# Projecting layer 3's context keys and values inside layer 1's context attention, and fetching them from DRAM batch by batch

## The chip, the cores and the metric

One Trainium2 chip; the kernel runs on one of its cores. The metric is the device time of one execution in microseconds, a median of several runs. A core has five engines, each with its own instruction queue that it works off in order: TensorE (PE, matrix products, whose weight loads the profile lists apart as PEld), VectorE (DVE), ScalarE (ACT), GpSimd (POOL) and SyncE (SP, which here only issues DMAs). TensorE reads from the on-chip memory SBUF and writes to the eight banks of PSUM; DVE and ACT copy results out of PSUM.

## The reference

The program is a decoder of four layers on x of 8 batches x 256 tokens x 256 features (float32). Each layer is x = layernorm(x + f(x)) three times: a self mixing, an attention to a context, and a feed-forward part. The context, `ctx_768`, is 8 batches x 120 tokens x 192 features and is the same for all layers; nothing in the network changes it. Two of the twelve parts matter here, and both attend to that context:

```python
def _L1_xattn_ref(...):   # 16 heads of 16, in layer 1
    q = x @ w_q + b_q;  k = context @ w_k + b_k;  v = context @ w_v + b_v
    ... softmax(q k^T / 4) v, then @ w_o + b_o

def _L3_xattn_ref(x, context, Wq, Wk, Wv, Wo, bo):   # 8 heads of 64, in layer 3
    q = (x @ Wq)...; k = (context @ Wk)...; v = (context @ Wv)...
    attn = softmax(q k^T * 64 ** -0.5)
    return (attn @ v) @ Wo + bo
```

Layer 3's keys and values depend on the context and on two weights (192 x 512 each) alone, so they can be computed at any time after these are loaded.

## The kernel before, in words

The parts run one after another over the same activations X (128 tokens by 256 features, 16 such tiles) and their transpose xT. `build` loads the weights of a part while the part ahead of it runs: there are two weight buffers that take turns, every load is issued on SP's queue, and it waits there until the buffer's last reader is done. The kernel is written as nested Python functions; the order in which they call an engine is the program order, and a scheduler may move an instruction in its engine's queue where it foresees a wait. So it is an in-order queue per engine that sets what runs when.

**Layer 1's context attention** (`l1_xattn`, from about 755 to 932 us of the profiled execution). `project` makes queries, keys and values of two batches at a time. Then `attention16` (L632) goes through the eight batches as a software pipeline. In the turn of batch b, TensorE computes the scores of b with keys as rows (`exps16`; ACT takes their exponentials, L556) and, in between, the scores of b + 1 with queries as rows (`largest16`; DVE takes their maxima into `low`, L501). The output projection of batch b - 1 lies between the first and second step. DVE and POOL then normalise batch b - 1 into X (L622, L167, L145, L147, L191), TensorE turns the maxima (L536, `lower16`) and the fresh X (L177, the turn), and `choose` computes the next part's gate logits and writes X to DRAM (L744, for the gathers of the mixture of experts that follows). Last come the weighted sums of b (L605). PSUM is handed out by `bank`, which goes round eight banks, six called `sc` and two `pt`. `attention16` has a hook, `ready`: three functions, of which the third gives, for a batch, an early, a late and a last step to be put into its turn. Layer 2's self attention uses it; layer 1's context attention doesn't.

**Layer 2's feed-forward part with layer 3 woven in** (`l2_ffn`, from about 1560 to 2440 us). Per batch, `experts` projects hidden units (PE), then gathers 64 x 128 rows of a table from DRAM by indirect DMAs that POOL issues one by one (L953), four at a time into one of four row buffers. DVE forms a dot product of each with X (L1480), ACT makes diagonal matrices of the weights (L1531) and PE adds the weighted rows up (L1532). At fixed places the loop takes one step, `next(later, None)`, of a chain of generators: the routing of the next batch, and layer 3's convolution and context attention (`convolve`, `attend`) of the batch before. What is left of the chain at the end of a batch is run before the batch is finished. The chain of the last batch, `convolve(7)` and `attend(7)`, is emitted after the loop and overlaps layer 3's feed-forward part (`fixed_point`), which ends the program. The weights of that last part (2 MB) are loaded on SP's queue between the loop and this chain.

`attend` is `context_batches` (L1609). Its first step for batch b adds the bias to X and computes keys and values: eight products of a 128 x 128 weight block with the 120 context columns into one PSUM tile, and two products of the context with 512 columns of weights into another. The second step copies them to SBUF, the keys on ACT (L1635), the values on DVE (L1636) beside a column of ones that POOL wrote once. Then follow queries, scores (L1656), exponentials, transposes (L1672), weighted sums with the column of ones giving the softmax's denominator (L1678), the output projection (L1696) and the norm.

The line numbers here and in the profile are those of the listing:

Of the kernel before, what the change touches and what calls it, by code (L numbers as in the profile page):

```python
# [11 lines left out]
F32 = mybir.dt.float32  # L12
# [8 lines left out]
P = 128  # L21
B, S, D = 8, 256, 256
NT = B * S // P
NTOK = B * S
SC, DC = 120, 192
# [17 lines left out]
class Net:  # L43
    def __init__(self, ctx: ExitStack, tc: tile.TileContext, ins, out):
        self.tc, self.nc, self.ins, self.out = tc, tc.nc, ins, out
        nc = self.nc
        self.const = ctx.enter_context(tc.tile_pool(name="const", bufs=1))
        self.wpool = ctx.enter_context(tc.tile_pool(name="weights", bufs=1))
        self.tmp = ctx.enter_context(tc.tile_pool(name="tmp", bufs=3))
        self.ps_t = ctx.enter_context(tc.tile_pool(name="ps_t", bufs=2, space=PSUM))  # L50

        self.ident = self.const.tile([P, P], F32, name="ident")
        make_identity(nc, self.ident)
        self.ones = self.const.tile([1, P], F32, name="ones")
        nc.gpsimd.memset(self.ones, 1.0)

        self.X = self.const.tile([P, NT, D], F32, name="X")
        self.xT = self.const.tile([P, 2, NTOK], F32, name="xT")
        self.xT4 = self.xT.rearrange("p c (t n) -> p c t n", n=P)
        for b in range(B):  # L60
            nc.sync.dma_start(
                self.X[:, 2 * b : 2 * b + 2, :],
                ins["x"][b].rearrange("(t p) d -> p t d", p=P),
            )
        self.cols = self.const.tile([P, ins["cols"].shape[1]], F32, name="cols")
        nc.scalar.dma_start(self.cols, ins["cols"])
        self.consts = self.const.tile([P, ins["consts"].shape[1]], F32, name="consts")
        nc.scalar.dma_start(self.consts, ins["consts"])
        self.earlier = self.const.tile([P, P], BF16, name="earlier")
        nc.vector.tensor_copy(self.earlier, self.cst("earlier"))  # L70
        self.causal = self.const.tile([P, P], BF16, name="causal")
        nc.vector.tensor_scalar(self.causal, self.cst("later"), -1e30, None, ALU.mult)

        self.later_k = self.const.tile([P, P], BF16, name="later_k")
        nc.vector.tensor_scalar(self.later_k, self.cst("sooner"), -1e30, None, ALU.mult)
        self.other = self.const.tile([P, P], BF16, name="other")
        nc.vector.tensor_scalar(self.other, self.cst("other"), -1e30, None, ALU.mult)
        self.ident_bf = self.const.tile([P, P], BF16, name="ident_bf")
        nc.vector.tensor_copy(self.ident_bf, self.ident)
        self.ones_bf = self.const.tile([P, P], BF16, name="ones_bf")  # L80
        nc.gpsimd.memset(self.ones_bf, 1.0)
        self.ctxT = self.const.tile([P, 2, NCTX], F32, name="ctxT")
        nc.scalar.dma_start(self.ctxT, ins["ctxT"].rearrange("p (c n) -> p c n", c=2))
        self.gate1 = self.const.tile([P, 2, 32], F32, name="gate1")
        nc.scalar.dma_start(self.gate1, ins["l1f_gate"].rearrange("p (c n) -> p c n", c=2))
        self.avg = self.const.tile([P, 2, B], F32, name="avg")

        self.x_max = self.const.tile([P, B], F32, name="x_max")
        self.w_scale = self.const.tile([P, len(L2X)], F32, name="w_scale")
        self.half = self.const.tile([P, 2], F32, name="half")  # L90
        nc.gpsimd.memset(self.half, -0.5)
        self.power = False
        dram = ctx.enter_context(tc.tile_pool(name="dram", bufs=1, space=bass.MemoryType.DRAM))

        self.xd1 = dram.tile([NTOK + 1, D], F32, name="xd1")

        self.yd1 = dram.tile([32 * 256 + 1, D], F32, name="yd1")
        self.one = self.const.tile([P, 1], F32, name="one")
        nc.gpsimd.memset(self.one, 1.0)
        self.wset = 0  # L100
# [609 lines left out]

    def load_l1_xattn(self):

        *w, spare = self.load(*((f"l1x_w{n}", 2) for n in "qkvo"), rows=("l1x_bv", "l1x_bo"), spare=16 * NT + 8)
        top = spare[:, : 16 * NT].rearrange("p (a t k) -> p a t k", a=2, k=8)
        self.top1, self.top1_i, self.w_sums = top[:, 0], top[:, 1].bitcast(U32), spare[:, 16 * NT :]
        return w

    def l1_xattn(self, w):
        nc = self.nc
        wq, wk, wv, wo, bv, bo = w  # L720
        with ExitStack() as ctx:
            work, low, vps = self.attn16_pools(ctx, "x1", SC, 1)
            bv, bo = self.everywhere(bv, work, "bv"), self.everywhere(bo, work, "bo")

            def project(b, vp):
# [27 lines left out]
                    nc.vector.max(self.top1[:, i, :], lg[:, j, :])  # L753
                    nc.vector.max_index(self.top1_i[:, i, :], self.top1[:, i, :], lg[:, j, :])

            self.attention16(project, low, vps, [SC], False, wo, bo, work, then=choose)

            o = 0
            for j, (_, k, n, _) in enumerate(L2X):
                n *= k // P  # L760
                for a in range(0, n, 2048):
                    m = min(2048, n - a)
# [653 lines left out]
    def l2_ffn(self, w):  # L1416


        tc = self.tc
        with ExitStack() as ctx:  # L1420
            w3 = self.load(
                ("l3a_win", 2), ("l3a_wout", 2), *((f"l3x_w{n}", 4 if n == "o" else 2) for n in "qkvo"),
                rows=("l3a_bout", "l3a_ln_w", "l3a_ln_b", "l3x_bo"),
            )
            win, wout, wq, wk, wv, wo, bout, ln_w, ln_b, bo = w3
            pool3 = ctx.enter_context(tc.tile_pool(name="a3", bufs=1))
            ps3 = ctx.enter_context(tc.tile_pool(name="a3p", bufs=2, space=PSUM))
            convolve = self.convolution_batches((win, wout, bout, ln_w, ln_b), pool3, ps3)
            attend = self.context_batches((wq, wk, wv, wo, bo), pool3, ps3)
            later = iter(())  # L1430
            with (
                tc.tile_pool(name="f2", bufs=1) as pool,
                tc.tile_pool(name="f2w", bufs=2) as work,
                tc.tile_pool(name="f2p", bufs=2, space=PSUM) as ps,
            ):
                experts = self.expert_batches(w, pool, work, ps)
                for b in range(B):
                    experts(b, later)
                    later = chain(convolve(b), attend(b))
            w4 = self.load(("l3f_w1", 2), ("l3f_w2", 8), rows=("l3f_b2",))  # L1440
            pool = ctx.enter_context(tc.tile_pool(name="f3", bufs=1))
            work = ctx.enter_context(tc.tile_pool(name="f3w", bufs=3))
            ps = ctx.enter_context(tc.tile_pool(name="f3p", bufs=2, space=PSUM))
            for _ in later:
                pass
            self.power = True
            self.fixed_point(w4, pool, work, ps)
# [161 lines left out]
    def context_batches(self, w, pool, ps):  # L1609

        nc = self.nc
        wq, wk, wv, wo, bo = w
        HD = 64
        v1 = pool.tile([SC, 8, HD + 1], F32, name="v1")
        nc.gpsimd.memset(v1[:, :, HD : HD + 1], 1.0)
        half = [slice(0, HD), slice(HD, 2 * HD)]
        out_bias = pool.tile([P, D], F32, name="out_bias")
        pp = ps.tile([P, D], F32, name="s")
# [3 lines left out]
        def batch(b):  # L1622
# [1 line left out]
            nc.vector.tensor_tensor(  # L1624
                z, self.X[:, 2 * b : 2 * b + 2, :], out_bias.unsqueeze(1).to_broadcast([P, 2, D]), ALU.add
            )
            ctxT = self.ctxT[:, :, b * SC : (b + 1) * SC]
            kT = pool.tile([P, 4, SC], F32, name="kT")
            pk = ps.tile([P, 4, SC], F32, name="s")
            for m in range(4):  # L1630
                self.mm(pk[:, m, :], [(wk[:, c, m * P : (m + 1) * P], ctxT[:, c, :]) for c in range(2)])
            pv = ps.tile([P, 512], F32, name="s")
            self.mm(pv[:SC], [(ctxT[:, c, :], wv[:, c, :]) for c in range(2)])
            yield
            nc.scalar.copy(kT, pk)  # L1635
            nc.vector.tensor_copy(v1[:, :, :HD], pv[:SC].rearrange("p (h d) -> p h d", d=HD))  # L1636
            qT = pool.tile([P, 4, S], F32, name="qT3")
            for m in range(0, 4, 2):
                pq = ps.tile([P, 2, S], F32, name="s")
# [594 lines left out]
```

## Time and profile before

| | |
|---|---|
| median of 3 runs | 2679.72 us (2677.69 to 2682.74) |
| the profiled execution | 2687.66 us, its span 2685.9 us |
| TensorE | 2173.3 us busy, 81% of the span, mean granted clock 0.884 |
| VectorE, ScalarE, GpSimd | 60%, 37%, 35% of the span |
| DMA traffic | 135.05 MB, 50 GB/s on average |
| layer 1's context attention, 755 to 932 us | PE 145.83 us busy of 177, granted clock 0.80 |
| the loop of layer 2's feed-forward part, 1600 to 2440 us | PE 657.60, DVE 564.54, POOL 514.74, ACT 344.09 us busy of 840; clock 0.88 |
| 2440 to 2530 us | PE 67.62 us busy of 90; clock 0.72 |

Busy times of TensorE come from modelled ends of pipelined products, and a product of float32 operands shows as two records. The granted clock is the share of full speed that the chip gave TensorE: at 0.50 a product takes twice as long. "Idle before" in a group of instructions is how long their engine had nothing to do just ahead of them, with the instruction that ended the wait. "Issue" is time in which the profile shows nothing that the engine waited for, and "remote" or "another core or an unknown queue" is a wait that ended by something not in the trace.

### The profile page before, as it was taken

The page shows a single profiled execution, that of the slowest core. Times are in us where ns is not written, and L with a number is a line of the kernel's source. Part 1 is how long each engine was busy: PE and PEld are TensorE (multiplying, and loading weights), DVE is VectorE, ACT ScalarE, POOL GpSimd, SP SyncE. Part 2 cuts the span into 40 slices and gives each one's busy share as a digit, 9 for nine tenths or more (in the row PEclk, how much of TensorE's full clock was granted, in tenths as well). Part 3 has the DMA queues.
Part 4 walks back from the last instruction along what each step waited for, and adds up shares of the span by engine and source line. Part 5 has one row for each costly group of instructions (what it writes and reads, how often), then busy time and mean ns, then how long its engine had stood idle before and what let it go on. Part 6 is the DMA issues. An engine that isn't in the chain of part 4 may idle for free.

```text
span 2685.9 us, 41132 instructions
## 1 busy us (share of the span) xinstructions
PE 2173.3 (81%) x14481; PEld 1569.7 (58%) x14481; DVE 1617.5 (60%) x5506; ACT 992.0 (37%) x2269; POOL 940.5 (35%) x986
## 2 busy tenths in 40 slices
PE   8989789699998689767886877788888778778796
PEld 5656678455565468434454355566667656555575
DVE  4664200566667576346667875757668676654675
ACT  2332233234333442123342433343445434342563
POOL 1021221311111134433210246665566555662122
PEclk9998799799988789878997888889889889887898
DMA  2001431200010137511001021111111111120000
GB/s 84 2 1 56 181 131 57 71 1 1 1 68 13 52 95 224 147 38 32 17 1 59 1 68 48 44 45 42 41 44 43 46 43 42 51 73 14 1 12 20
DMA packets 84173, 135.05 MB, mean 50 GB/s; under 512 B 33445, under 2 KB 53045, under 8 KB 82048
## 3 DMA queue, kind: packets, MB, share of 16 engines
q0 software_dynamic: 52288, 79.27, 10.0%
q1 hardware_dynamic: 28924, 49.45, 5.6%
q10 hardware_dynamic: 2756, 3.72, 0.4%
q8 instruction: 115, 1.88, 0.3%
q14 instruction: 90, 0.74, 0.1%
HBM read 242.90 MB, written 17.70 MB: 97 GB/s over the span
## 4 chain that ended last, share of the span: by engine, by line
PE 38%; DVE 21%; issue 9%; POOL 4%; ACT 4%; another core or an unknown queue 4%; DMA 3%; POOLq 0%; ACTq 0%; DVEq 0%
PE po L1532 5%; PE pp L136 5%; PE s L136 4%; PE sc L136 4%; PE ph L136 2%; DVE low L517 2%; PE sc L484 2%; DMA xe<-xd,take 2%; PE pt L136 2%; DVE low L501 2%; PE sc L605 1%; DVE junk L1480 1%; DVE X L191 1%; PE s L1678 1%
## 5 line engine op out<-in xcount | busy, mean ns | idle before, releaser
L953 POOL DMA_INDIRECT rows<-in_l2f_table_dram,index x512 | 532.8, 1041 | 340.8 <-issue 122.0
L1532 PE MATMUL po<-rows,diag 128*128 128x256 f32 x768 | 226.8, 431 | 92.9 <-ACT diag L1531 62.1
L1480 DVE SCALAR_TENSOR_TENSOR junk<-rows,X 128x256 f32<-128x256 f32 x512 | 214.5, 419 | 57.2 <-DMA rows<-in_l2f_table_dram,index 34.1
L1532 PEld LDWEIGHTS po<-rows,diag 128*128 128x128 f32 x768 | 150.0, 209 | 144.4 <-ACT diag L1531 75.9
L136 PE MATMUL pp<-xT,w 128*128 128x256 f32 (+1 forms) x672 | 196.2, 429 | 26.8 <-issue 21.4
L592 POOL TENSOR_TENSOR aT<-sides,inv 128x256 f32<-128x256 f32 x64 | 46.8, 731 | 431.6 <-DVE sides L590 316.6
L136 PE MATMUL ph<-xeT,we 128*128 128x128 f32 x1248 | 182.7, 289 | 18.3 <-DMA we<-in_l0f_experts_dram,wrow 15.1
L136 PEld LDWEIGHTS ph<-xeT,we 128*128 128x128 f32 x1248 | 168.2, 199 | 38.6 <-DMA we<-in_l0f_experts_dram,wrow 16.4
L1531 ACT ACTIVATE diag<-ident,dots 128x128 f32<-128x128 f32 x384 | 133.8, 394 | 114.7 <-PE po L1532 51.7
L177 PE MATMUL pt<-ident,X 128*128 128x128 f32 x352 | 77.4, 337 | 116.9 <-DVE X L191 93.3
L136 PEld LDWEIGHTS pp<-xT,w 128*128 128x128 f32 x672 | 137.3, 213 | 57.5 <-issue 27.3
L178 ACT COPY xT<-pt 128x512 f32<-128x512 f32 x88 | 51.5, 587 | 302.5 <-PE pt L177 219.0
L953 POOL DMA_INDIRECT xe<-xd,take x87 | 85.2, 979 | 205.3 <-PE pt L968 80.6
L177 PEld LDWEIGHTS pt<-ident,X 128*128 128x128 f32 x352 | 49.6, 165 | 153.1 <-issue 53.1
L136 PE MATMUL py<-we,hT 128*128 128x256 f32 x496 | 129.1, 384 | 0.9 <-DVE hT L1097 0.9
L1074 DVE TENSOR_TENSOR y<-py,we 128x256 f32<-128x256 f32 x23 | 9.8, 424 | 197.6 <-PE py L136 197.6
L556 ACT ACTIVATE e<-sc 128x512 f32<-128x512 f32 (+1 forms) x154 | 81.4, 601 | 103.0 <-PE sc L484 73.9
L1068 ACT ACTIVATE hT<-ph,we 128x128 f32<-128x128 f32 x184 | 65.8, 367 | 119.6 <-PE ph L136 84.9
L484 PE MATMUL sc<-kv,qv 32*128 32x128 f32 (+2 forms) x1448 | 104.2, 320 | 1.7 <-DVE qv L694 0.6
L191 DVE TENSOR_SCALAR X<-z,ln_mv,rs_y 128x256 f32<-128x256 f32 x176 | 68.1, 429 | 58.8 <-POOL rs_y L147 58.4
L136 PE MATMUL s<-xT,w 128*128 128x256 f32 x256 | 72.3, 444 | 38.3 <-issue 26.4
L484 PEld LDWEIGHTS sc<-kv,qv 32*128 32x128 f32 x1448 | 80.2, 190 | 31.2 <-issue 25.9
(535 smaller groups left out, 5204.9 us busy)
## 6 DMA issues: line engine op xcount, KB each, us to landing
we<-in_l1f_experts_dram SPq DMA_DIRECT2D x32, 384.0 KB
yd<-y SPq DMA_DIRECT2D x32, 256.0 KB
rows<-in_l2f_table_dram,index POOLq DMA_INDIRECT x512
w<-in_l2x_w_dram SPq DMA_DIRECT2D x1, 4096.0 KB
yd<-y SPq DMA_DIRECT2D x23, 128.0 KB
X<-in_x_dram SPq DMA_DIRECT2D x8, 256.0 KB
xd<-X ACTq DMA_DIRECT2D x8, 256.0 KB
xd<-X SPq DMA_DIRECT2D x8, 256.0 KB
```

Source lines behind the costliest of these rows:

```text
L136: self.nc.tensor.matmul(out, lhsT=lhsT, rhs=rhs, start=n == 0, stop=n == last and bias is None)
L177: nc.tensor.transpose(pt[:, c, j, :], self.X[:, i0 + j * step, c * P : (c + 1) * P], self.ident)
L191: nc.vector.tensor_scalar(self.X[:, i, :], z[:, j, :], mv[:, j, 0:1], r[:, j : j + 1], ALU.subtract, ALU.mult)
L484: nc.tensor.matmul(sc[: shape[0], part], lhsT=lhsT, rhs=rhs, start=mask is None, stop=True, skip_group_check=True)
L501: nc.vector.tensor_reduce(low5[:, r, :, :, 0], sc, AX.X, ALU.max, negate=True)
L517: nc.vector.tensor_reduce(low4[:, r, :, 0], sc, AX.X, ALU.max, negate=True)
L556: lambda r, sc: nc.scalar.activation(e0[m][:n0, r], sc, AF.Exp),
L953: self.nc.gpsimd.indirect_dma_start(out=out, out_offset=None, in_=table, in_offset=bass.IndirectOffsetOnAxis(ap=index, axis=0), **({} if r ...
L1068: nc.scalar.activation(hT[:, g + f, :], ph[:, f, :], AF.Gelu, bias=b1[:, g + f : g + f + 1])
L1480: nc.vector.scalar_tensor_tensor(junk, row, 1.0, self.X[:, i, :], ALU.mult, ALU.mult, accum_out=out)
L1531: nc.scalar.activation(diag, self.ident, AF.Copy, scale=dots[:, k : k + 1])
L1532: nc.tensor.matmul(po, lhsT=diag, rhs=rows[:, k, D:], start=False, stop=g + k == H * K - 2)
```

## The change

The keys and values of layer 3 are no longer computed in `attend`. Their two weights (512 KB each) are loaded with the weights of layer 1's context attention instead of with layer 3's. In the turn of each batch of layer 1's context attention, as the late step of the hook, a new function `context3` computes the same ten products, copies the keys on ACT and the values on DVE, and writes both to two DRAM buffers from SP's queue (245,760 bytes and 249,600 bytes). The ones beside the values are written by POOL into two buffers once, and travel along. In layer 3, the first step of `attend` fetches both tiles of its batch from DRAM on SP's queue in place of the ten products, and the second step loses both copies.

```diff
+        self.k3 = dram.tile([B, P, 4 * SC], F32, name="k3")
+        self.v3 = dram.tile([B, SC, 8 * 65], F32, name="v3")
...
-        *w, spare = self.load(*((f"l1x_w{n}", 2) for n in "qkvo"), rows=("l1x_bv", "l1x_bo"), spare=16 * NT + 8)
+        *w, spare = self.load(
+            *((f"l1x_w{n}", 2) for n in "qkvo"), ("l3x_wk", 2), ("l3x_wv", 2),
+            rows=("l1x_bv", "l1x_bo"), spare=16 * NT + 8,
+        )
...
+            v3 = [work.tile([SC, 8, 65], F32, name=f"v3{n}", bufs=1) for n in range(2)]
+            for t in v3:
+                nc.gpsimd.memset(t[:, :, 64:], 1.0)
...
+            def context3(b):
+
+                ctxT = self.ctxT[:, :, b * SC : (b + 1) * SC]
+                pk = self.bank([P, 4, P])[:, :, :SC]
+                for m in range(4):
+                    self.mm(pk[:, m, :], [(wk3[:, c, m * P : (m + 1) * P], ctxT[:, c, :]) for c in range(2)])
+                kT = work.tile([P, 4, SC], F32, name="k3")
+                nc.scalar.copy(kT, pk)
+                nc.sync.dma_start(self.k3[b], kT.rearrange("p m s -> p (m s)"))
+                pv = self.bank([P, 512])
+                self.mm(pv[:SC], [(ctxT[:, c, :], wv3[:, c, :]) for c in range(2)])
+                v = v3[b % 2]
+                nc.vector.tensor_copy(v[:, :, :64], pv[:SC].rearrange("p (h d) -> p h d", d=64))
+                nc.sync.dma_start(self.v3[b], v.rearrange("p h d -> p (h d)"))
+
+            def inside(b):
+                return lambda: None, lambda: context3(b), lambda: None
...
-            self.attention16(project, low, vps, [SC], False, wo, bo, work, then=choose)
+            self.attention16(
+                project, low, vps, [SC], False, wo, bo, work, then=choose,
+                ready=(lambda: None, lambda: None, inside),
+            )
...
-                ("l3a_win", 2), ("l3a_wout", 2), *((f"l3x_w{n}", 4 if n == "o" else 2) for n in "qkvo"),
+                ("l3a_win", 2), ("l3a_wout", 2), ("l3x_wq", 2), ("l3x_wo", 4),
...
-        v1 = pool.tile([SC, 8, HD + 1], F32, name="v1")
-        nc.gpsimd.memset(v1[:, :, HD : HD + 1], 1.0)
...
-            ctxT = self.ctxT[:, :, b * SC : (b + 1) * SC]
             kT = pool.tile([P, 4, SC], F32, name="kT")
-            pk = ps.tile([P, 4, SC], F32, name="s")
-            for m in range(4):
-                self.mm(pk[:, m, :], [(wk[:, c, m * P : (m + 1) * P], ctxT[:, c, :]) for c in range(2)])
-            pv = ps.tile([P, 512], F32, name="s")
-            self.mm(pv[:SC], [(ctxT[:, c, :], wv[:, c, :]) for c in range(2)])
+            nc.sync.dma_start(kT, self.k3[b].rearrange("p (m s) -> p m s", m=4))
+            v1 = pool.tile([SC, 8, HD + 1], F32, name="v1")
+            nc.sync.dma_start(v1, self.v3[b].rearrange("p (h d) -> p h d", h=8))
             yield
-            nc.scalar.copy(kT, pk)
-            nc.vector.tensor_copy(v1[:, :, :HD], pv[:SC].rearrange("p (h d) -> p h d", d=HD))
             qT = pool.tile([P, 4, S], F32, name="qT3")
```

In the queues of the built program, TensorE's ten products stand in each turn of layer 1's context attention behind the last of the scores and ahead of the four turns of the maxima (L536), which in the program before had been spread around the turn of X (L177). On SP's queue the two writes of a batch stand ahead of X's write of the batch before it (L744) or near it, and in layer 3 the fetches of batch 7 stand behind the 2 MB of weights for the last part.

## The prediction

> **What bounds the kernel now.** I read first the chain of work that ended last, to see which engines the time hangs on; then the busy time by stretch, for the two parts that the change touches; then the timeline of TensorE in each, for what is idle where work is added and what stands on the chain where work is taken out.
>
> ```profile
> PE 38%; DVE 21%; issue 9%; POOL 4%; ACT 4%; another core or an unknown queue 4%; DMA 3%; POOLq 0%; ACTq 0%; DVEq 0%
> ...
> 1600.00:2440.00 840.00, 657.60 (x2928) 507.51 (x2926) 564.54 (x2770) 344.09 (x899) 514.74 (x495) 0.88 0.17 47
> ```
>
> TensorE carries 38% of the chain, more than any other engine. The second line is the gather loop (length; PE, PEld, DVE, ACT, POOL busy; clock; DMA share; GB/s): PE is busy 78% of it. POOL's 64 gathers per batch of about 1.04 us, with 0.30 us between them, are 86 us of the 107 to 123 us that a batch takes, so POOL is not the bound.
>
> What is moved, seen in batch 0 (PE's timeline, then the two copies by line, min/median/max in ns):
>
> ```profile
> 1736.05 1.94 PE L136 MATMUL s<-ctxT,w 128*128 128x120 f32 x16
> 1737.83 1.88 PE L136 MATMUL s<-w,ctxT 128*120 128x512 f32 x4
> ...
> L1635 ACT COPY kT<-s x8: 559/559/560, 1739.6 to 2523.5; 128x480 f32<-128x480 f32 x8
> ...
> L1636 DVE COPY v<-s x8: 680/692/692, 1741.8 to 2526.1; 120x512 f32<-120x512 f32 x8
> ```
>
> The ten products run from 1736.05 to 1737.83 + 1.88 = 1739.71: 3.66 us at full clock. They lie on the chain itself (start, us, what):
>
> ```profile
> 2188.98 3.69 PE s L136 x20
> ...
> 2303.42 3.69 PE s L136 x20
> ...
> 2426.28 5.28 PE s L136 x20
> ...
> 2519.80 6.29 PE s L136 x20
> ```
>
> Where they arrive, PE stands idle once per batch, ahead of the turn of X, and then runs slow:
>
> ```profile
> 796.63 0.78 PE L177 MATMUL pt<-ident,X 128*128 128x128 f32 x4 [1.46 <-DVE X L191]
> ...
> 816.19 1.12 PE L177 MATMUL pt<-ident,X 128*128 128x128 f32 x4 [3.37 <-DVE low L501]
> ...
> 814.00:816.00 2.00, 0.00 (x0) 0.00 (x0) 2.00 (x5) 0.00 (x0) 0.00 (x0) 0.76 0.32 109
> 816.00:818.00 2.00, 1.81 (x8) 1.81 (x9) 0.71 (x3) 0.59 (x1) 0.00 (x0) 0.50 0.11 35
> 818.00:820.00 2.00, 2.00 (x6) 0.97 (x5) 1.40 (x2) 0.00 (x0) 0.00 (x0) 0.50 0.00 0
> 820.00:822.00 2.00, 2.00 (x17) 1.48 (x20) 0.52 (x6) 0.21 (x1) 0.00 (x0) 0.50 0.00 0
> 822.00:824.00 2.00, 2.00 (x24) 0.97 (x20) 0.97 (x3) 0.06 (x1) 0.00 (x0) 0.50 0.00 0
> 824.00:826.00 2.00, 2.00 (x13) 1.20 (x6) 1.59 (x5) 0.42 (x1) 0.73 (x1) 0.68 0.00 0
> 826.00:828.00 2.00, 2.00 (x9) 1.23 (x8) 1.32 (x5) 1.36 (x3) 0.00 (x0) 1.00 0.00 0
> ```
>
> PE waits 1.46 us or 3.37 us in turn (batch pairs differ in where DVE's maxima lie), and after the gap at 814 the clock stays at 0.50 until about 825.
>
> **The added work, in layer 1's context attention.** Per batch 3.66 us of PE, 0.56 of ACT, 0.69 of DVE and two SP issues of 0.36 us (the row of L744).
>
> PE. The ten products stand just where the gap is. In the turns with the long gap (three) they cost 3.66 - 3.37 = 0.3 us. In those with the short one (three) the four turns of the maxima now stand ahead of X's turn, and need DVE's last maximum, which the trace has done at 799.07; the products end at 794.90 + 3.66 = 798.56, so 0.5 us of waiting comes on top: 3.66 + 0.5 - 1.46 = 2.7. In batch 0 the place is in a stretch at clock 0.50 without a gap: between 3.7 and 7.3, I take 5. In batch 7 the gap is 2.36 us: 1.3. Sum 3 x 0.3 + 3 x 2.7 + 5 + 1.3 = 15.3 us.
>
> The clock. From 796 to 904 us, counting each 2 us stretch's busy time times (1 - clock), PE loses 18 us of work to slow spells, each right behind a gap. Filled gaps should avoid part of them. The Trainium skill (TensorE: Matmul & The Clock Gate, Part 1) says that the clock halves after an idle window of about 3.4 us and returns after about 3.4 us of work. By that rule only the three long gaps go cold, for 3.4 us at half speed each: 3 x 1.7 = 5 us to win, and the part costs 10. The row shows more: a gap of 1.46 us is followed by half clock too (from 798), and the return takes 7 to 10 us. I take half of the 18, 9 us, so the part costs +6. The same rule speaks against the change further on: fewer products in the gather loop leave PE colder.
>
> The copies: ACT's stands behind the exponentials and ahead of xT's copy, which waits for PE anyway; DVE's behind the maxima, while PE is busy with L536. Hidden by PE's own work; bare, 8 x 1.25 = 10 us. SP's writes: X's write (L744) queues near them, but only the gathers of the next part read it, from 965 us, 37 us after the last is issued at 928. POOL's two 0.11 us memsets come before the first batch. The weights' 1 MB is issued at 271 us, behind l1x's 1 MB, which took 270 to 274; DMA is idle until the first expert's fetch at 281.73, so it is through by 278.
>
> Bounds: -3 (all slow spells gone: 15.3 - 18) to +33 (nothing hidden: 8 x 3.66 + 3.7 for the cold batch).
>
> **The removed work, in layer 3.** The chain holds of the products 3.69 us each in batches 3 to 5, 3.05 in batch 1, 1.9 (as an unknown wait) in batch 0 and 2.7 (as "issue") in batch 2: 18.7 us, with about 1.8 us of the copies on the chain 20.5. In the tail, at low clock, 5.28 + 6.29 = 11.6 us. A shorter chain meets the next longest one. In the loop that is ACT, whose longest waits are of another kind:
>
> ```profile
> ACT qT L1473 <- remote: 38.8, 4, 12.2
> ...
> ACT xT L178 <- remote: 31.8, 5, 9.8
> ```
>
> These waits of 5 to 12 us stop PE and DVE as well, end by nothing in the trace, and are not shortened. I take 70% in the loop (14 us): PE feeds itself from one product to the next there, and POOL has 20 us per batch to spare. In the tail I take 60% (7 us), since the next products lose the warm-up that these gave: the clock returns at 2525, at their end. Together -21; bounds -2 and -32.
>
> **The fetches.** Sixteen of 0.25 MB; at the pace of 270 to 274 us (1 MB in 4 us) 1 us each, with a latency as that of the gathers from DRAM on the chain, 3 to 5 us. SP's queue holds nothing else from 1563 to 2399. A fetch waits until the batch before has read its tile: keys are last read at 1800 and next at 1899, values at 1811 and 1907; the nearest pair is 2371 and 2454, the values of batches 5 and 6. Cover of over 80 us against 5. Batch 7's stand behind the last part's weights, which wait for L1513 until 2399, but their own tiles come free only at 2471 and 2478 and are used from 2552. Nothing waits. Without this cover each would cost about 5 us. They share the DMA engines with gathers that DVE waits for (29.7 us in all over the loop): between 0 and 16 us, I take 1. Layer 3's weights shrink by 1 MB at 1557; the first gather at 1576.8 waits for its index, so 0.
>
> **Sum.** +6 - 21 + 1 = -14, against the profiled execution: span 2685.9 to 2672. It took 2687.66 us, 1.8 outside the span, and lies 8 us above the median; the difference carries over: 2679.7 - 14 = 2666 us.
>
> **The rivals.**
> 1. *A wait takes the gap's place (slower).* Between L484 and L177, X's turn now stands behind all four turns of the maxima; if the maxima slip by as much as the products take, the gap stays and the 3.66 us come on top. For it: DVE reduces X and the maxima in one queue, ending 0.5 us behind the products already. Against it: DVE has no other work then. Price +33, less 21: +12, 2692. It decides once a batch costs more than 21 / 8 = 2.6 us net.
> 2. *The removed products were filler.* PE is idle 182 us of the loop, and if ACT's waits or the row buffers set the pace only a third of 32 comes back: -10 + 6 + 1 = -3, 2677, no change.
> 3. *The clock heals.* All slow spells of the attention go and the chain gives 28 us: -3 - 28 = -31, 2649.
> 4. *The fetches collide with gathers*: +15 on the forecast, 2681; in the trace gathers have DMA engines busy 17%, so this is small and goes with rival 2.
>
> **How the numbers follow.** Forecast (2653 to 2674) 0.44; rival 1 0.29; rivals 2 and 4 0.15; rival 3 0.12. 0.2% or 5.4 us is about what a measurement can tell from no change. Faster: forecast and rival 3, 0.56; same 0.15; slower 0.29. The range leaves one in ten on each side: below, rival 3 without its end, 2645; above, rival 1 with part of its worse half, 2697.
>
> **What would show it.** In the changed profile: the wait of L177 for X or the maxima, 20.7 us in all between 750 and 930, falls below 8; the clock of that stretch rises from 0.80 to 0.85 or more, and it grows by 0 to 12 us. L1656 and L1678 never wait for a DMA. The loop from the first gather to the drain shortens by about 14 us, with ACT's remote waits as long as now; the tail by 7. Wrong if the attention grows by over 20 us with L536 waiting for L501 in every turn, or the loop keeps its length.

## The result and the profile after

The kernel after takes 2673.82 us against 2691.98 us of the kernel before, both medians of 20 runs: a ratio of 0.9933, 95% interval 0.9915 to 0.9951, or 18 us faster (13 to 23). The prediction was 2666 us from 2679.7, 14 us faster. The profiled executions differ by 13.3 us of span, 2685.9 to 2672.6. Cut at fixed instructions, the difference lies here (ahead of the first stretch the kernel after is 1.0 us later, where the two differ only in loading two weights):

| stretch (first and last instruction) | before | after | difference | predicted |
|---|---|---|---|---|
| layer 1's context attention (`zero` to the first routing sum) | 177.8 | 171.9 | -5.9 | +6 |
| from there to the first `qT` of layer 2's feed-forward part | 627.5 | 629.9 | +2.4 | 0 |
| from there to the last table gather (the loop) | 876.4 | 863.8 | -12.6 | -14, +1 for the fetches |
| from there to the last output DMA (the tail) | 243.4 | 245.3 | +1.9 | -7 |

The total came close because two errors of opposite sign nearly met: the attention was costed 12 us too dear, the tail 9 us too cheap.

First TensorE's timeline in the turn whose gap was shown before (start, us, what; the wait ahead of it in brackets):

```profile
794.40 1.35 PE L487 MATMUL sc<-kv,qv 32*128 32x120 f32 x32
795.68 2.04 PE L139 MATMUL sc<-ctxT,w 128*128 128x120 f32 x16
797.56 1.88 PE L139 MATMUL pt<-w,ctxT 128*120 128x512 f32 x4
799.28 0.27 PE L539 MATMUL pt<-ident,low 128*128 128x128 f32 x1
799.97 0.55 PE L539 MATMUL pt<-ident,low 128*128 128x128 f32 x3 [0.41 <-DVE low L504]
800.56 0.66 PE L180 MATMUL pt<-ident,X 128*128 128x128 f32 x4
```

The ten products fill the gap. X's turn (L180, before L177) waits for nothing; the wait for the last maximum that the prediction put at 0.5 us is 0.41. Of all waits of TensorE between 750 and 930 us, those of X's turn were 20.7 us in the kernel before (10.6 for X, 10.1 for a maximum) and are now one line (us in total, times, longest; two lines before, then the one after):

```profile
PE pt L177 <- DVE X L191: 10.6, 6, 3.4
PE pt L177 <- DVE low L501: 10.1, 3, 3.4
...
PE pt L180 <- DVE X L194: 3.9, 2, 3.4
```

Now four of the stretches of 2 us around the long gap shown before, where the clock was at 0.50 from 816 us on (length; PE, PEld, DVE, ACT, POOL busy; clock; DMA share; GB/s), and the whole attention, before and after:

```profile
814.00:816.00 2.00, 2.00 (x17) 1.75 (x16) 1.21 (x3) 1.14 (x3) 0.71 (x1) 1.00 0.00 0
816.00:818.00 2.00, 1.59 (x6) 0.54 (x5) 2.00 (x5) 0.21 (x1) 0.00 (x0) 1.00 0.71 252
818.00:820.00 2.00, 2.00 (x20) 1.23 (x19) 1.80 (x3) 0.59 (x1) 0.00 (x0) 1.00 0.35 83
820.00:822.00 2.00, 2.00 (x30) 1.37 (x29) 0.56 (x1) 0.21 (x1) 0.00 (x0) 1.00 0.13 48
...
755.40:933.20 177.80, 145.54 (x1302) 99.64 (x1301) 115.84 (x317) 66.15 (x131) 29.62 (x43) 0.80 0.09 33
756.40:928.30 171.90, 150.40 (x1461) 107.84 (x1460) 120.72 (x326) 70.52 (x139) 29.51 (x45) 0.93 0.16 57
```

The clock of the attention rose from 0.80 to 0.93. Counted as in the prediction (busy time times 1 minus clock, over 2 us stretches), TensorE lost 30.9 us of work to a slow clock in the kernel before and 9.5 after. It idled 32.3 us (177.80 - 145.54) and 21.5 us. Its work at full clock, busy time less that loss, grew from 114.6 to 140.9 us. So by this count 26.3 us of added work stand against 21.4 us less lost and 10.8 us less idle, which gives the -6.

In the loop, the same 840 us as shown before, and ScalarE's longest waits there:

```profile
1600.00:2440.00 840.00, 660.76 (x2825) 506.55 (x2826) 567.63 (x2800) 339.66 (x901) 515.32 (x497) 0.87 0.18 50
```

```profile
ACT silu L1126 <- remote: 63.0, 11, 9.6
ACT xT L181 <- remote: 44.1, 6, 9.7
```

The clock of the loop is 0.87 instead of 0.88; that the loop is 12.6 us shorter is read from the cuts in the table. ScalarE's waits that end by nothing in the trace did not shorten: all of this kind are 157 us, 137 before, on other instructions. The 12.6 us were won in spite of 20 us more of these waits, so one pair of profiles does not fix this number. The fetches are waited for by nobody: of the lines that read them, the scores wait for these (us, times) and for no DMA,

```profile
L1679 PE MATMUL s<-kT,qT x256: 271/272/567, 1776.8 to 2558.2; 64*128 64x120 f32 x128
...
  ACT qT L1672: 15.5, 11
  issue: 5.4, 15
  ACT dots L1555: 0.7, 1
  ACT diag L1561: 0.3, 1
```

and the weighted sums (L1701) for no DMA either. The chain of work on the page after covers only a few per cent of the span, so it can't be set against the one before; the stretches and waits carry the comparison.

### The profile page after: what moved, and what is told of

The parts are those of the page before. It is cut to its first block, busy times and chain, and to the rows that moved or that the text cites. A ratio compares the mean times of both kernels' runs of the same rounds, so it can differ in the third digit from the quotient of the medians.

```text
span 2672.6 us, 41230 instructions
## 1 busy us (share of the span) xinstructions
PE 2166.4 (81%) x14481; PEld 1569.6 (59%) x14481; DVE 1619.4 (61%) x5506; ACT 986.1 (37%) x2268; POOL 943.1 (35%) x987
## 2 busy tenths in 40 slices
DMA packets 88638, 142.99 MB, mean 54 GB/s; under 512 B 33941, under 2 KB 55589, under 8 KB 86512
## 3 DMA queue, kind: packets, MB, share of 16 engines
q0 software_dynamic: 52288, 79.27, 10.1%
## 5 line engine op out<-in xcount | busy, mean ns | idle before, releaser
L1562 PE MATMUL po<-rows,diag 128*128 128x256 f32 x768 | 233.3, 438 | 97.5 <-ACT diag L1561 73.0
L139 PEld LDWEIGHTS ph<-xeT,we 128*128 128x128 f32 x1248 | 168.5, 199 | 39.2 <-DMA we<-in_l0f_experts_dram,wrow 17.1
L180 PE MATMUL pt<-ident,X 128*128 128x128 f32 x352 | 77.7, 339 | 116.9 <-DVE X L194 102.6
L180 PEld LDWEIGHTS pt<-ident,X 128*128 128x128 f32 x352 | 50.1, 167 | 153.1 <-DVE X L194 59.6
L139 PE MATMUL sc<-xT,w 128*128 128x512 f32 x216 | 101.6, 619 | 1.3 <-ACT xT L181 1.3
```

What stands on the lines that cost most here:

```text
L139: self.nc.tensor.matmul(out, lhsT=lhsT, rhs=rhs, start=n == 0, stop=n == last and bias is None)
L180: nc.tensor.transpose(pt[:, c, j, :], self.X[:, i0 + j * step, c * P : (c + 1) * P], self.ident)
L1562: nc.tensor.matmul(po, lhsT=diag, rhs=rows[:, k, D:], start=False, stop=g + k == H * K - 2)
```

## The experiments

The kernel before had another median in each of three groups of runs (2567.93 us on chip 2; 2704.16 and 2695.93 us on chip 0), so ratios count, and profiled stretches are compared within a group. The three profiles without added products in the attention show 177.8, 174.3 and 173.3 us for it; those with one set in the gap of X's turn, and batch 0 as in the change, 171.4 to 173.0 (eight profiles). The three differ by 4.5 us among themselves, the eight by 1.6. The loop differs more from profile to profile: the kernels without the products in it show 857 to 872 us in the two groups on chip 0.

### Each part alone, the gap filled with waste, and the products elsewhere

**The added part alone.** Layer 3's weights are loaded in both places, and layer 3 computes its own keys and values as before; those in DRAM are not read.

```diff
             w3 = self.load(
-                ("l3a_win", 2), ("l3a_wout", 2), ("l3x_wq", 2), ("l3x_wo", 4),
+                ("l3a_win", 2), ("l3a_wout", 2), *((f"l3x_w{n}", 4 if n == "o" else 2) for n in "qkvo"),
...
             kT = pool.tile([P, 4, SC], F32, name="kT")
-            nc.sync.dma_start(kT, self.k3[b].rearrange("p (m s) -> p m s", m=4))
...
+            pk = ps.tile([P, 4, SC], F32, name="s")
...
```

> The added part alone: layer 1's context attention computes and writes layer 3's keys and values, and nobody reads them; layer 3 computes its own as before. Theory (the products fill the gap and keep TensorE's clock up): the attention, 177.8 us before, takes 171 to 174, the loop 860 and the tail 243 as before, the whole 0 to 7 us less than before, as some of the gain is given back before the loop. The term of the prediction (+6): attention 184, whole +6. Rival (the gain in the traces is the chance of one execution): attention 184 to 200, whole +6 to +22.

Measured: 2565.83 us against 2567.93, ratio 0.9990 (0.9978 to 1.0003). Attention 172.9 us at clock 0.91, tail 241.1. The added products (8 x 3.66 = 29.3 us) cost nothing, and may win up to 6 us. That rules out the prediction's +6 for this part (interval -5.6 to +0.8).

**The removed part alone.** Layer 1's attention has no added products; the two DRAM buffers are filled once, and layer 3 fetches from them.

```diff
             nc.sync.dma_start(self.xd1[0:1, :], zero)
+            v3 = work.tile([SC, 8 * 65], F32, name="v3", bufs=1)
+            nc.gpsimd.memset(v3, 1.0)
+            for b in range(B):
+                nc.sync.dma_start(self.k3[b], self.ins["l3x_wk"][:, : 4 * SC])
+                nc.sync.dma_start(self.v3[b], v3)
```

> The removed part alone: layer 1's attention as before; the DRAM buffers are filled once with a weight's columns and with ones, by 16 writes ahead of the attention's first batch, and layer 3 fetches these in place of its keys and values (its attention to the context is then another function). Theory: attention 176 to 180, loop 845 to 848 against 860, tail 243 to 246, whole 11 to 16 less than before. Prediction: loop 846, tail 236, whole -20. Rival (the products were filler): loop 855 to 860, whole -5 to 0.

Measured: 2552.84 us, ratio 0.9937 (0.9919 to 0.9955), -16 us (-21 to -12). Attention 174.3 us at 0.83, as it has no products to fill the gap; loop 753.9 us against 766.9 with the added part alone; tail 242.8 against 241.1. With the part above this makes -19 for the change, where the whole change measured -18 and, in the second group, -17: the parts add up. The tail gained nothing here either.

**The gap filled with waste.** In the kernel before:

```diff
+            def filler(b):
+                ctxT = self.ctxT[:, :, b * SC : (b + 1) * SC]
+                pk = self.bank([P, 4, P])[:, :, :SC]
+                for m in range(4):
+                    self.mm(pk[:, m, :], [(wq[:, c, (m % 2) * P : (m % 2 + 1) * P], ctxT[:, c, :]) for c in range(2)])
+                pv = self.bank([P, 2, 256])
+                for n in range(2):
+                    self.mm(pv[:SC, n], [(ctxT[:, c, :], wv[:, c, :]) for c in range(2)])
...
+                ready=(lambda: None, lambda: None, inside),
```

> The kernel before with waste: in the place of the late step, ten products of the attention's own weights with the context, of the same column count as the added ones, whose result nobody reads; no copies, no writes, nothing removed anywhere. Theory (TensorE's clock is what is won): the attention gets shorter all the same, 170 to 174 against 177.8, with a clock above 0.88 instead of 0.80. By the term of the prediction (half of the slow spells lost): 184, clock 0.85. If the clock is not what is won: 180 to 207, up to eight times 3.66 us more.

Measured: 2564.10 us, ratio 0.9990 (0.9978 to 1.0001); attention 172.2 us. The whole attention of the removed part alone and of this kernel, of the same group:

```profile
756.30:930.60 174.30, 141.40 (x1301) 96.69 (x1301) 116.41 (x316) 66.09 (x131) 29.91 (x43) 0.83 0.13 45
```

```profile
753.00:925.20 172.20, 152.01 (x1493) 115.12 (x1493) 115.18 (x314) 66.28 (x131) 29.42 (x42) 0.91 0.09 34
```

Some 29 us of products that nobody needs leave the attention no longer, and rather shorter: the clock goes from 0.83 to 0.91 and the loss to slow clock from 26.7 to 11.5 us, the idle time from 32.9 to 20.2. Copies, writes and weights of the change play no part in that, since this kernel has none of them.

**The products as the early step**, ahead of the turn's scores.

```diff
-                return lambda: None, lambda: context3(b), lambda: None
+                return lambda: context3(b), lambda: None, lambda: None
```

> As the kernel after, but the ten products as the early step, ahead of the turn's first scores; the order around the turn of X is then that of the kernel before, and the gap ahead of it stays. Theory: the clock of the attention stays at 0.80 or 0.81 and each batch pays in full, so attention 200 to 210 against 171.9 in the kernel after, whole 27 to 38 more than the kernel after, so +10 to +22 against before. Rival (products are cheap there wherever they stand, since DVE and ACT set the pace): attention 172 to 182.

Measured: 2566.63 us, ratio 0.9993 (0.9983 to 1.0002), attention 186.6 us at clock 0.88. The same products cost 13.7 us more here than in the gap (172.9), and take back all that layer 3 gives. The gap stays, as TensorE's waits in the attention show:

```profile
PE pt L180 <- DVE X L194: 10.2, 5, 3.4
PE pt L539 <- DVE low L504: 7.9, 2, 4.0
PE pt L180 <- DVE low L504: 2.3, 1, 2.3
```

The direction is the theory's, the size is not: 200 to 210 us was expected, with the clock at 0.80. Batch 0's products now stand in the prologue's waits, and the clock stayed at 1.00 up to 795 us, where the kernels before and after lose 5 to 8 us of work. That suggested the last experiment below.

### The kernels again, batch 7, and a second set of products

> The kernel before once more, for its stages on the chip of these runs. Both theories: the same time. If its ScalarE waits that end by nothing in the trace are the chip's and not the program's, the loop up to the last gather takes about 765 us as in the run of the added part alone; if they are the program's, 860. The attention: 174 to 178.

Measured: 2703.13 us against 2704.16; attention 173.3 us at 0.82, X's turn waiting 19.8 us; loop 884.5, tail 246.1. ScalarE's waits that end by nothing are back (more on them below).

> The kernel after once more, beside it. If the two parts add up as they did alone, the attention is 1 to 6 us shorter than in the kernel before, the part from the first routing of layer 2's feed-forward on 8 to 12 us shorter, the whole 13 to 19 less (0.993 to 0.995). Rival (the parts overlap, as the loop is colder and the attention warmer by the same sum): 5 to 10 less.

Measured: ratio 0.9938 (0.9915 to 0.9961), attention 171.4 us at 0.93, loop 869.6 (-14.9), tail 245.7 (-0.4). The parts add up. The stretch between attention and loop is again 2.6 us longer (634.3 against 631.7), and longer in the other two runs of this group too (634.2 and 636.2 us), but not in the group where those ScalarE waits are absent (622 to 623 in all four). The third group has no profile of the kernel before to compare with. What makes it longer was not found.

**Batch 7 computed in layer 3**, whose products stand in the tail:

```diff
+            if b in (7,):
+                ...
+                pk = ps.tile([P, 4, SC], F32, name="s")
+                for m in range(4):
+                    self.mm(pk[:, m, :], [(wk[:, c, m * P : (m + 1) * P], ctxT[:, c, :]) for c in range(2)])
...
+            else:
+                nc.sync.dma_start(kT, self.k3[b].rearrange("p (m s) -> p m s", m=4))
+                nc.sync.dma_start(v1, self.v3[b].rearrange("p (h d) -> p h d", h=8))
```

> As the kernel after, but batch 7's keys and values, whose products stand behind the gather loop, are computed in layer 3 as before; its weights are loaded there again. Theory (TensorE has these 6 us to spare while VectorE norms X for the next turn, and they keep it warm): the same time as the kernel after, -3 to +3, with the stretch behind the last gather 241 to 246. By the prediction's step (60% of the 6.29 us on the path): +4. If they are wholly on the path: +6.

Measured: ratio 0.9925 (0.9896 to 0.9955), 3 us below the kernel after with overlapping intervals, tail 247.6 against 245.7 in one profile each. So the removal is worth at most 2 us there. TensorE's timeline shows why, in the kernel after of the same group and then with the products:

```profile
2513.67 1.22 PE L141 MATMUL s<-w,ones 1*128 1x256 f32 x2
...
2543.92 1.11 PE L180 MATMUL pt<-ident,X 128*128 128x128 f32 x4 [1.59 <-DVE X L194]
```

```profile
2518.51 3.48 PE L139 MATMUL s<-ctxT,w 128*128 128x120 f32 x16
2521.83 1.88 PE L139 MATMUL s<-w,ctxT 128*120 128x512 f32 x4
...
2544.37 0.87 PE L180 MATMUL pt<-ident,X 128*128 128x128 f32 x4 [2.64 <-DVE X L194]
```

Ahead of X's turn VectorE norms X, in one queue with the last part's steps over 128 x 1024 elements (0.7 to 1.2 us each). With the products, which start at 2518.51 as soon as the convolution's last product is done, X's turn comes 25.9 us later. Without them that last product ends at 2513.67 + 1.22 = 2514.89, and X's turn comes 29.0 us later. Taking out 5 us of TensorE's work brought the turn no nearer.

VectorE's queue shows where it went. In the four profiles with the products in the tail (two of the kernel before, this one, and that of the products left unread below), 12 of those steps stand between the convolution and X, 11.4 us, and X's turn comes 25.3 to 27.0 us after the convolution. In four without them (three of the kernel after, and that of the threefold fetches below), 15 steps stand there, 14.7 to 15.1 us, and the turn comes 28.5 to 29.1 us after it. Without the removed products TensorE goes on at once with those of the last part, at a low clock (6.42 us for 16 records at clock 0.57 in the kernel after of this group, 3.62 us for the same at clock 1.00 behind the products), and VectorE takes more of the last part's steps ahead of X.

**A second set of products in the attention.**

```diff
+                again = self.bank([P, 4, P])[:, :, :SC]
+                for m in range(4):
+                    self.mm(again[:, m, :], [(wk3[:, c, m * P : (m + 1) * P], ctxT[:, c, :]) for c in range(2)])
+                again = self.bank([P, 512])
+                self.mm(again[:SC], [(ctxT[:, c, :], wv3[:, c, :]) for c in range(2)])
```

> As the kernel after, with the ten products of each batch computed twice in the attention (the second result is not read). Theory (one set fills the gap, the second finds none): each further set costs its full 3.66 us, the attention takes 26 to 32 us more than in the kernel after, 198 to 203, and the clock stays above 0.9. Rival (VectorE and ScalarE set the pace of the attention and TensorE has room left): +5 to +15, as in the run with the early step.

Measured: ratio 1.0028 (1.0011 to 1.0045), 24 us more than the kernel after; attention 193.5 us, +22.1, clock 0.95. The first set costs -1 to -6 us, the second +22: the gap holds one set. Each set is 29.3 us, so a quarter of the second was still hidden; 26 to 32 were expected, and the theory missed that quarter.

### The removed products by themselves, more fetches, and batch 0 earlier

> The kernel after again, as the measure for the three others on the chip of these runs: attention 171 to 173, ratio to the kernel before 0.993 to 0.995.

Measured: ratio 0.9943 (0.9915 to 0.9970), attention 173.0 us at 0.91.

**The products stay in layer 3, unread.**

```diff
             nc.sync.dma_start(v1, self.v3[b].rearrange("p (h d) -> p h d", h=8))
+            ctxT = self.ctxT[:, :, b * SC : (b + 1) * SC]
+            pk = ps.tile([P, 4, SC], F32, name="s")
+            for m in range(4):
+                self.mm(pk[:, m, :], [(wk[:, c, m * P : (m + 1) * P], ctxT[:, c, :]) for c in range(2)])
+            pv = ps.tile([P, 512], F32, name="s")
+            self.mm(pv[:SC], [(ctxT[:, c, :], wv[:, c, :]) for c in range(2)])
             yield
```

> As the kernel after, but layer 3 computes the ten products of each batch too, into the same two PSUM tiles, and nobody reads them; the keys and values still come from DRAM, and the two copies stay away. It parts the removed products from the removed copies. Theory (the products are on the path in the loop, and warm it): 6 to 12 us more than the kernel after, nearly all that the removal had won. Rival (the copies and the PSUM tiles they held were the cost): 0 to 4 more.

Measured: 2691.75 us, 12 more than the kernel after; ratio to the kernel before 0.9992 (0.9973 to 1.0012). The profile has it all in the loop (888.0 us against 863.3, more than the medians bear; ScalarE's waits that end by nothing are some 40 us longer in it) and none in the tail (244.5 against 245.7). The products, and at most in a small part the copies, were what the loop paid for: 12 us of the 29.3 that they take, where the removed part alone won 16 (12 to 21).

**Each fetch three times**: a loop of three around the two fetch lines.

> As the kernel after, but each fetch of keys and values in layer 3 is issued three times, into the same tiles. Theory (nobody waits for a fetch, 80 us of cover, and the load on the DMA engines costs the gathers next to nothing): -2 to +3 us. Rival (fetches collide with the gathers, 15 us for one set): +15 to +30.

Measured: 2680.56 us, 1 more than the kernel after, at 150.92 MB instead of 142.99. The fetches now wait for one another on SP's queue, and no engine for them:

```profile
SPq L1658 <- DMA kT<-k: 22.7, 10, 4.1
SPq L1659 <- DMA v<-v: 19.3, 9, 3.2
```

These waits, 4.1 us at most, each end when the fetch ahead into the same tile has landed. One set of fetches costs nothing that can be measured.

**Batch 0's products as the early step**, the others as in the kernel after.

```diff
-                return lambda: None, lambda: context3(b), lambda: None
+                none = lambda: None
+                return (lambda: context3(b), none, none) if b == 0 else (none, lambda: context3(b), none)
```

> As the kernel after, with batch 0's products moved from the late to the early step, where they fall into the two waits of 1.37 us of the prologue's maxima turns; in the kernel after TensorE runs at half clock behind these for about 9 us. Theory (a filled gap keeps the clock up): the attention 4 to 8 us shorter than in the kernel after, 163 to 168, clock 0.95 or more, whole 2 to 8 less than the kernel after. Rival (the clock's gain in the attention was order or chance): attention 171 to 173.

Measured: 2662.25 us, ratio 0.9901 (0.9873 to 0.9930), 17 us less than the kernel after in the medians, where 2 to 8 were expected. The profile has 7.2 us in the attention, 165.8 us at clock 0.96. The loop is shorter too (857.4 against 863.3), within what profiles of the same loop differ by, and so is the work ahead of the attention (8.3 us), where the two programs do the same; so the other 10 us of the medians have no cause shown. TensorE's timeline in the prologue, and then that of the profiled execution of the kernel after,

```profile
761.42 0.33 PE L539 MATMUL sc<-ident,low 128*128 128x128 f32 x1 [1.37 <-DVE low L504]
761.59 1.94 PE L139 MATMUL sc<-ctxT,w 128*128 128x120 f32 x16
763.37 1.02 PE L139 MATMUL sc<-w,ctxT 128*120 128x512 f32 x2
764.23 0.49 PE L539 MATMUL sc<-ident,low 128*128 128x128 f32 x3
```

```profile
764.49 0.33 PE L539 MATMUL sc<-ident,low 128*128 128x128 f32 x1 [1.37 <-DVE low L504]
766.18 1.63 PE L487 MATMUL pt<-kv,qv 32*128 32x120 f32 x6 [1.37 <-DVE low L504]
```

have one wait of 1.37 us and two, with 0.33 us of work between them. The clock there, in the same order:

```profile
762.00:764.00 2.00, 2.00 (x16) 1.70 (x16) 1.62 (x3) 0.43 (x1) 0.00 (x0) 1.00 0.00 0
764.00:766.00 2.00, 2.00 (x14) 0.81 (x12) 1.24 (x2) 0.13 (x1) 0.00 (x0) 1.00 0.32 123
766.00:768.00 2.00, 2.00 (x50) 1.62 (x42) 0.93 (x3) 1.05 (x3) 0.00 (x0) 1.00 0.23 46
```

```profile
766.00:768.00 2.00, 1.82 (x7) 1.61 (x8) 0.69 (x2) 0.00 (x0) 0.00 (x0) 0.50 0.00 0
...
772.00:774.00 2.00, 2.00 (x26) 1.98 (x25) 0.61 (x2) 1.74 (x4) 0.00 (x0) 0.50 0.00 0
```

Within the first 40 us the loss to slow clock falls from 4.7 us to none (against the third run of the kernel after). This kernel is faster than the kernel before; against the kernel after, the intervals of the two ratios just overlap (0.9873 to 0.9930 and 0.9915 to 0.9970).

## Why the prediction was right, point by point

**PE in the attention: the mechanism right, the clock's term mis-sized.** The gap was filled, X's turn waits 3.9 us instead of 20.7 (below 8 was forecast), the new wait is 0.41 us (0.5), the clock 0.93 (0.85 or more). The step that failed is "I take half of the 18, 9 us". Between 796 and 904 us the 17.8 us of loss fell to 2.6, so 15 of the 18 were won, and over the whole attention 21.4. The filled-gap sum of 15.3 was near: 26.3 us of work less 10.8 us of idle time gives 15.5. So the term was 15.5 - 21.4 = -6 in this execution. Part of it was the execution: the attention without the products showed 177.8, 174.3 (with the removed part alone) and 173.3 us, so the term is -1 to -6, and +6 is ruled out. The choice of half had no row behind it; every slow spell between 796 and 904 us stood right behind a gap that the products were to fill, and the row would have supported nearly the whole. The reading of the spells was too regular as well: of the three gaps of 1.46 us, the one at 837.6 us was followed by no slow spell (the two lines from 838 to 842 us below, at clock 1.00), and the spell behind the gap at 852.5 us lasted 3.4 us, not 7 to 10.

```profile
838.00:840.00 2.00, 1.47 (x7) 0.93 (x6) 2.00 (x5) 1.33 (x3) 0.72 (x1) 1.00 0.00 0
840.00:842.00 2.00, 2.00 (x32) 1.56 (x32) 1.77 (x5) 0.00 (x0) 0.31 (x1) 1.00 0.00 0
```

The Trainium skill's rule (TensorE: Matmul & The Clock Gate, Part 1), a cooling window of about 3.4 us, would have given +10, further off: two of the three gaps of 1.46 us were followed by half clock too, for 6.8 and 10.2 us; with them filled, 3.4 us of these spells were left.

**The copies, SP's writes and the weights: right.** Waste in the gap, without any of them, gives the attention the same length (172.2 against 172.9 us).

**The removal in the loop: right, within what can be told.** 14 us was forecast, and 12.6 and 14.9 measured up to the last gather in two pairs of profiles. By the medians the products alone are worth 12 us, and the part alone 16 (12 to 21), loop and tail together; the 21 forecast for both is at the edge of that. The 70% had no row behind it, so that it came out is in part luck. ScalarE's waits without a visible end did not shorten, as forecast.

**The removal in the tail: wrong.** "In the tail I take 60% (7 us)" measured +1.9 and -0.4 us, and the profiles with the products put back 1.9 us longer (batch 7's alone) and 1.2 us shorter (all of them). The chain of waits did list the products there, 6.29 us of them, and the argument was that they lie on the path. But a chain goes back through the instruction ahead on the engine even where that engine could have done its work later. Beside it VectorE was norming X, and X's turn came when VectorE was done. The 40% held back for a lost warm-up had a reason: the last part's products, now first, did run at the low clock. What the prediction did not look at was VectorE's queue, which took three more of the last part's steps ahead of X. The next wait behind the products would have told that they might not bind. X's turn waited for VectorE even with the products there, in the kernel before already:

```profile
2546.76 0.87 PE L177 MATMUL pt<-ident,X 128*128 128x128 f32 x4 [2.64 <-DVE X L191]
```

**The fetches: right** (+1 forecast; two more sets of them on top cost 1).

**The rivals.** Rival 1, the gap stays and the products come on top, is what the early step shows: attention +12 against the removed part alone, and no gain left in the whole. The danger was real, and the place decided it. Rival 2, that a third of the 32 us comes back in layer 3, was half right: 12 to 16 came back, nearer to its 10 than to the 21 of the forecast, because of the tail. That the result isn't rival 2's is the attention's doing. Rival 3 was right in the attention's term alone (its -3). Between attention and loop 2.4 us went to a cause that stays open.

## What to carry to other kernels

Work that is off the critical path belongs where TensorE waits anyway, and the credit for it is more than the gap: a filled gap also saves the slow clock behind it, and here that was worth more than the gap's own length (21.4 us against 10.8). The same products cost -1 to -6 us in the gap and 12 us a few microseconds earlier, so look at the order in the queue before costing a move, and count slow stretches and the gap ahead of each as one item. For removed work, ask which other engine reaches the next point where both must be done, and when; a chain of waits that lists the work doesn't say.

## What the runs showed of the hardware that was not expected

- The granted clock moves in steps of one length. In the trace of the kernel before it changes 133 times, and the stretches between two changes are whole multiples of 3.413 us. In its context attention the stretches at 0.50 last 3.4, 6.8, 10.2 and 17.1 us. In the longest (763.86 to 780.93 us) TensorE waits for nothing over 0.3 us from 765.28 us on, and yet the clock takes 15.7 us more to return.
- Waits shorter than that can be followed by half clock, but need not be. Ahead of X's turn, in two profiles of the kernel before, the removed part alone and the early step, there are twelve waits of 1.45 to 1.47 us: eight were followed by half clock within 2 us of their end, four were not. In all twelve profiles with both waits of 1.37 us in the prologue half clock followed (about 9 us of busy time in the kernel after); in the two with products in place of the second, the clock stayed at 1.00. That it takes both waits is not shown: in the kernel before the clock fell at 763.86 us, just ahead of the second. What decides, the place of a wait in those steps or the work around it, was not tested.
- Useless products are free in the gap and bring the clock up (0.83 to 0.91 with waste).
- ScalarE's waits that end by nothing in the trace, 137 us in the loop of the kernel before, do not come from the change. In the group of runs where the kernel before takes 2568 us instead of 2680 to 2704, on chip 2, the four traces have none, and the loop, with the products in it, takes 762 to 767 us instead of 876 to 885. Whether the chip makes the difference, one group there cannot tell. What the waits are, no trace says; transfers of program code are an unlikely cause, as the loops of the kernel before and of the added part alone both have 70 packets of them, and the latter none of these waits. About 110 us of the loop go with these waits, six times what the change brought.
